# Adjacency block sums made one node tile at a time, and a range check on reciprocals once per batch

## The chip, the core and the metric

The kernel runs on one core of one Trainium2 chip. The metric is the device time of one execution in microseconds, as the median of several runs. A core has five engines with instruction queues of their own: TensorE (PE in the profile; PEld is its loading of weights), VectorE (DVE), ScalarE (ACT), GpSimd (POOL) and SyncE (SP), which issues nearly all DMA transfers here. Each works through its queue in order and waits on semaphores for the others.

## What is computed

Sixteen batches of 1024 nodes with 256 channels go through an attention layer whose queries come from a weighted adjacency, and then through two graph convolutions. Cut to what matters:

```
c    = mean of x over channels
A    = |abs(sigmoid(c_j - c_i) - 0.5) - 0.5| * 2          # likeness of nodes
q    = relu((x^T @ (adj * A_sym)) * para)                  # queries
k, v = x @ kv_w
x1   = layernorm(x + softmax(q k^T * scale) v)             # 4 heads of 64
h    = relu(x1 w1_loop + adj (x1 w1_neigh) + b1)
h    = relu(h w2_loop + adj (h w2_neigh) + b2)
out  = layernorm(x1 + (x1 + h) / 2)
```

All is float32. The adjacency, 1024 x 1024, is the same for all batches.

## The kernel before

**Tiles.** A node tile is 128 nodes; there are eight. Most work tiles are "rows" of 128 partitions x 1024 floats, from a pool of 25 with a tag of their own (`row_tile`). The transposed adjacency is kept as four blocks of 512 x 512. Blocks (0,0), (1,0) and (1,1) stay on chip in `half_adj`, four node tiles of 512 columns each (index k, 0 to 3). Block (0,1) starts out in two row tiles (`rows01`), two node tiles in each, and is stored to memory in batch 1.

**Stages of a batch.** The attention of a batch has four units (two pairs of heads x two halves of the query nodes). A unit computes scores (TensorE, line 596), exponentials (ScalarE, line 599), the running sum of the eight exponential tiles (VectorE, lines 603 and 605), transposes and reduces that sum to `den_part` (lines 607 and 609), and multiplies with the values (TensorE, line 616). `add(u)` then folds the denominators with a small product into PSUM (`den_ps`, line 628, on TensorE), takes reciprocals (line 632), updates a running minimum and maximum of all denominators (lines 633 and 634), scales the output and adds it to x (lines 636 to 639). The minimum and maximum are tested at the very end of the kernel: only if a denominator has left a safe range are all batches redone in a slower, guarded way.

Between the units of batch b stands other work in an order that is written out by hand: after unit 0 the inner product of the convolution of batch b-1 (`gap0`: `c1.inner`, t_ps, line 714), then `att.add(0)`, so `den_ps` follows t_ps on TensorE; after unit 1 the convolutions themselves (`gap1`); after unit 2 the convolution's end (`gap2`). After unit 3 come the queries, keys and values of batch b+1 (`q.step`, line 549; `kv.run`, lines 399 to 434), then the normalization of batch b (`norm.scale`, `norm.spread`), then the next batch's unit 0.

**Block sums.** From batch 2 on, two convolutions of neighbouring batches are done together as one blocked matrix product with seven products instead of eight (`Joined`). Its adjacency operands include four sums of blocks (1, 3, 2, 4, in order of making), which do not change and are made once. `adj_sums(rows01, h)`, lines 196 to 208, makes them for two node tiles at a time: four subtractions of 128 x 1024 on VectorE, each with a store of 512 KB to the memory blocks `far_adj`. It is called twice, both times in batch 1: with h = 0 in the convolution, as a function called after the first four products (line 1020), and with h = 1 behind the next batch's keys and values and ahead of `norm.scale` (line 1109). From batch 2 on the sums are fetched back in every batch.

**Getting the blocks.** The adjacency's node tiles are loaded in blocked form by `adj_blocked` (line 210) and transposed by `turn_adj` (line 951) on VectorE, two transpositions of 512 columns for each tile: tiles 0, 1 and 2 in the opening, while TensorE computes the first queries, and 3 to 7 at the end of batch 0. Tiles k and 4 + k are both needed before the sums for index k can be made. In the opening GpSimd also scales five weight tiles (lines 150 and 152).

**Queues.** Every engine follows the order of the program. SyncE issues a DMA only when its data is ready and its buffer free, and what is behind it waits. The last queries' step of a batch (`q.step(3)`) needs the weighings and sums of `q.pair(3)`, which VectorE makes after `att.add(3)`.

Of the kernel before, what the change touches and what calls it, by code (L numbers as in the profile page):

```python
# [18 lines left out]
def kernel(  # L19
# [31 lines left out]
    nc = tc.nc  # L51

    B, N, C = x.shape
# [10 lines left out]
    EPS2 = EPS / 2.25  # L64
    QSCALE = (1.0 + 1e-06) / (math.sqrt(HD) + 1e-06)

    DEN_MIN = 1e-25
    DEN_MAX = 1e28
    ROWS = 25
    S = 32  # L70
    NB = N // S
# [27 lines left out]
    def row_tile(name):  # L99
        return work.tile([P, N], F32, tag="row", name=name, bufs=ROWS)  # L100
# [62 lines left out]
    for a in range(1, Q):  # L163
        nc.vector.tensor_copy(fold[:, a, :], fold[:, 0, :])

    den_min = const.tile([P, N // S], F32, name="den_min")
    nc.gpsimd.memset(den_min, 1.0)
    den_max = const.tile([P, N // S], F32, name="den_max")
    nc.gpsimd.memset(den_max, 1.0)

# [19 lines left out]
    def of_rows(rows, k):  # L190
        return rows[k // 2][:, ts(k % 2, FB)]
# [1 line left out]
    def adj_block(i, j, k, rows01):  # L193
        return of_rows(rows01, k) if (i, j) == (0, 1) else half_adj[i, j][:, k, :]

    def adj_sums(rows01, h):

        names = (1, 3, 2, 4)
        w11, w21, w22 = (half_adj[ij][:, 2 * h:2 * h + 2, :] for ij in ((0, 0), (1, 0), (1, 1)))
        w12 = rows01[h].rearrange("p (k n) -> p k n", k=2)  # L200
        t = {n: row_tile(f"adjT_{n}_{h}") for n in names}
        v = {n: t[n].rearrange("p (k n) -> p k n", k=2) for n in names}
        nc.vector.tensor_sub(v[1], w12, w11)
        nc.vector.tensor_sub(v[3], w22, w12)
        nc.vector.tensor_sub(v[2], w22, v[1])
        nc.vector.tensor_sub(v[4], w21, v[2])
        for n in names:
            nc.sync.dma_start(out=far_adj[n][h], in_=t[n])

    def adj_blocked(mt):  # L210
        t = row_tile(f"adjB_{mt}")
        for a in range(Q):
            nc.sync.dma_start(
                out=t[a * S:(a + 1) * S, :].rearrange("k (bn r) -> k bn r", r=S),
                in_=adj[:, mt * P + a * S:mt * P + (a + 1) * S].rearrange("(bn k) r -> k bn r", k=S))
        return t
# [39 lines left out]
    def join(part):  # L256
        nc.vector.tensor_add(part[:, 0, :], part[:, 0, :], part[:, 1, :])
# [317 lines left out]
    class Attention:  # L575
# [6 lines left out]
        def __init__(self, b, xB, qT, kT, v):  # L582
            self.b, self.xB, self.qT, self.kT, self.v = b, xB, qT, kT, v
            self.part, self.o = {}, {}

            self.sums = small.tile([P, NC, NB], F32, tag="sums", name=f"sums_{b}", bufs=2)

        def scores(self, u):
# [33 lines left out]
        def add(self, u):  # L622

            b, (pair, j) = self.b, UNITS[u]
            half = FB // S
            pd = bank_psum(f"den_ps_{b}_{u}")
            den = pd[:, 0:2 * half]
            nc.tensor.matmul(den, fold.rearrange("p a k -> p (a k)"), self.part.pop(u), start=True, stop=True)  # L628
            rden = small.tile([P, half], F32, tag="rden", name=f"rden_{b}_{u}", bufs=2)
            for s in range(2):  # L630
                rows = slice(s * HD, (s + 1) * HD)
                nc.vector.reciprocal(rden[rows, :], den[rows, ts(s, half)])
            nc.vector.tensor_tensor(den_min, den_min, den, ALU.min)
            nc.vector.tensor_tensor(den_max, den_max, den, ALU.max)
            o = by_node(self.o.pop(u))
            nc.vector.tensor_mul(o, o, rden.unsqueeze(2).to_broadcast([P, half, S]))
            dst = by_node(self.xB[pair][:, ts(j, FB)])
            nc.vector.tensor_add(dst, dst, o)
            nc.vector.tensor_reduce(self.sums[:, pair, ts(j, half)], dst, AX.X, ALU.add)
            if u == len(UNITS) - 1:  # L640
                join(self.sums)

    def safe_attention(b, xb, qT, kT, v):

# [271 lines left out]
    def run():  # L916
# [14 lines left out]
        sum_key_weights()  # L931
        q.load_para()
        blocked = load_blocked(1, "1")
        tiles = {mt: adj_blocked(mt) for mt in range(3)}
        load_weights()

        def first_weights():
# [22 lines left out]
        for t in range(NT):  # L960
            if t + 3 < NT:
                q.weigh(t + 3)
            q.step(t)
            if t == 4:
                xB = load_blocked(0, "a0")
                ready = {}
                ready["xT"] = channel_major(blocked, "xT_1")
                turn_adj(range(3))
        qT = q.end()
        convs = {}  # L970
        coming = None
        for b in range(B):
# [25 lines left out]
            def weigh_first():  # L998
                q.times_adj(0)
                q.times_adj(TJ)  # L1000
                q.right(0)

            def gap1():
                for t in (0, TJ):
                    q.load(t)
                if both:
                    both.fetch(1, 4)
                    both.run({1: (lambda: q.left(nc.gpsimd),),
                              2: (lambda: att.add(1),),
                              6: (lambda: q.likeness(0), lambda: c3 and c3.moments()),  # L1010
                              7: (lambda: q.likeness(TJ),),
                              5: (weigh_first,),
                              4: (lambda: c3 and c3.finish(out[b - 3]),),
                              3: (c1.turn_blocks,)})
                else:
                    q.left(nc.gpsimd)
                    for t in (0, TJ):
                        q.likeness(t)
                    store("01", rows01)
                    c1.first(rows01, lambda: (att.add(1), adj_sums(rows01, 0), weigh_first()))  # L1020
                    c1.turn_blocks()

            def gap2():
# [36 lines left out]
            if more and not c1:  # L1060
                xT = ready["xT"]
                for t in range(3, NT):
                    q.load(t)
                for t in range(3, NT):
                    q.likeness(t)
                tiles[3] = adj_blocked(3)
                q.times_adj(3)
                q.step(0)
                q.times_adj(4)
                q.step(1)  # L1070
                att.add(3)
                for mt in range(4, NT):
                    tiles[mt] = adj_blocked(mt)
                q.load_para()
                q.times_adj(5)
                q.step(2)
                q.step(3)
                norm.mean()
                q.times_adj(6)
                q.times_adj(7)  # L1080
                q.step(4)
                norm.squares()
                norm.sum_squares()
                q.step(5)
                q.step(6)
                norm.variance()
                xB = load_blocked(b + 1, f"a{b + 1}")
                q.step(7)
                qT = q.end()
                load_next()  # L1090
                norm.scale()
                norm.spread()
                turn_adj(range(3, NT))
                kT, v = keys(b + 1, xT), values(b + 1, xT)
            elif more:
# [12 lines left out]
                if not c2:  # L1108
                    adj_sums(rows01, 1)
                norm.scale()  # L1110
                norm.spread()
            else:
                c2.load_h1()
                c2.load_x()
                both.fetch(2, 3)
                c1.inner()
                both.left(nc.gpsimd)
                both.fetch(1, 4)
                both.run({1: (lambda: att.add(3),), 2: (norm.mean, norm.squares, norm.sum_squares), 7: (norm.variance,),
                          5: (norm.scale, norm.spread)})  # L1120
                c1.turn(0)
                c2.last()
                c1.turn(1)
# [20 lines left out]

    good = small.tile([P, 2], F32, tag="good", name="good", bufs=1)
    ext = small.tile([P, 2], F32, tag="ext", name="ext", bufs=1)
    nc.vector.tensor_reduce(ext[:, 0:1], den_min, AX.X, ALU.min)
    nc.vector.tensor_reduce(ext[:, 1:2], den_max, AX.X, ALU.max)
    nc.vector.tensor_single_scalar(good[:, 0:1], ext[:, 0:1], DEN_MIN, op=ALU.is_ge)
    nc.vector.tensor_single_scalar(good[:, 1:2], ext[:, 1:2], DEN_MAX, op=ALU.is_le)  # L1150
    nc.vector.tensor_mul(good[:, 0:1], good[:, 0:1], good[:, 1:2])
    pn = bank_psum("good_ps")
    nc.tensor.matmul(pn[0:1, 0:1], good[:, 0:1], ones_sb, start=True, stop=True)
# [56 lines left out]
```

## Time and profile before

| what | value |
|---|---|
| median of three runs | 2174.52 us (2174.29 to 2175.86) |
| the profiled execution | 2174.29 us |
| its span, first to last instruction | 2172.4 us |
| busy: TensorE, VectorE, ScalarE, GpSimd | 99%, 87%, 47%, 17% of the span |
| mean granted TensorE clock | 0.998 |
| HBM read and written | 238.16 MB and 46.46 MB, 131 GB/s |
| sum of exponentials (lines 603 and 605) | 571.3 us of VectorE |
| minimum and maximum (lines 633 and 634) | 12.1 and 11.5 us of VectorE, 64 each |
| block sums (lines 203 to 206) | 10.7 us of VectorE, 8 instructions |

The page gives busy time per engine, then the span in 40 slices, DMA queues, the chain of work that ended last, and the costliest groups of instructions. A timeline lists instructions in order of time: start, length, engine, line, operation, output and inputs, shapes, and in brackets how long the engine idled before it and who ended that. Times in a timeline are counted from the start of the span. [...]A list of waits gives the total, the number and the longest. The granted clock is the share of TensorE's full clock that it was given.

### The profile page before, as it was taken

The numbers are of one execution on the slowest core, as the hardware profiler recorded it, in microseconds if no ns is written. First come the engines' busy times: TensorE is split into PE (matmuls) and PEld (weight loads), VectorE is DVE, ScalarE is ACT, GpSimd is POOL, SyncE is SP. The second block draws the span as 40 slices with busy tenths as digits, with TensorE's granted clock in tenths as the row PEclk, the third lists the DMA queues.
The fourth block names the chain that finished last, engine by engine and source line by source line (L and its number), as shares of the span: only waits on it lengthen the run. The fifth ranks groups of instructions, "written<-read, shape, count | busy, mean of one in ns | idle before, by whom it ended". The sixth has DMA issues, their size and how long they took to land.

```text
span 2172.4 us, 23124 instructions
## 1 busy us (share of the span) xinstructions
PE 2155.6 (99%) x8054; PEld 1026.6 (47%) x8054; DVE 1893.7 (87%) x2431; ACT 1027.7 (47%) x1346; POOL 368.2 (17%) x210
## 2 busy tenths in 40 slices
PE   9999999999999999999999999999999999999997
PEld 5344444544444444444444445454454544544354
DVE  4978988898998989989899898999989899898965
ACT  4744545535455453445444454445543445535411
POOL 1011120221303113031120301203022130221021
PEclk9999999999999999999999999999999999999999
DMA  9393563746557374583655626556374653743342
GB/s 230 95 139 116 140 175 89 119 153 122 149 125 144 124 121 155 125 164 102 113 158 130 163 88 114 172 122 155 97 111 166 121 155 113 121 149 82 117 138 96
DMA packets 610619, 286.22 MB, mean 132 GB/s; under 512 B 504640, under 2 KB 569024, under 8 KB 610496
## 3 DMA queue, kind: packets, MB, share of 16 engines
q1 hardware_dynamic: 610224, 284.15, 55.0%
q8 instruction: 65, 1.06, 0.2%
q14 instruction: 58, 0.48, 0.1%
q10 hardware_dynamic: 272, 0.52, 0.1%
HBM read 238.16 MB, written 46.46 MB: 131 GB/s over the span
## 4 chain that ended last, share of the span: by engine, by line
PE 97%; DVE 2%; ACT 0%; DMA 0%; issue 0%; SPq 0%; POOLq 0%; DVEq 0%; POOL 0%
PE s L596 20%; PE av L616 20%; PE hu_ps L875 17%; PE g_ps L549 16%; PE v_ps L363 5%; PE k_ps L408 4%; PE t_ps L714 3%; PE h_ps L782 3%; PE hu_ps L721 2%; PE g_ps L476 2%; PE h_ps L783 2%; DVE acc L605 1%; PE h_ps L736 1%; PE u_ps L765 1%; PE k_ps L353 1%; PE den_ps L628 0%
## 5 line engine op out<-in xcount | busy, mean ns | idle before, releaser
L599 ACT ACTIVATE pr<-s 128x1024 f32<-128x1024 f32 x512 | 476.4, 1054 | 180.0 <-PE s L596 179.9
L605 DVE TENSOR_TENSOR acc<-acc,pr 128x1024 f32<-128x1024 f32 x384 | 494.4, 1288 | 40.7 <-DVE acc L605 0.5
L596 PE MATMUL s<-qT,kT 64*128 64x512 f32 x2048 | 458.8, 598 | 0.7 <-ACT qT L483 0.7
L616 PE MATMUL av<-pr,v 128*64 128x512 f32 x2048 | 453.6, 595 | 0.0
L596 PEld LDWEIGHTS s<-qT,kT 64*128 64x128 f32 x2048 | 191.8, 186 | 237.1 <-ACT pr L599 109.5
L616 PEld LDWEIGHTS av<-pr,v 128*64 128x64 f32 x2048 | 141.4, 137 | 300.0 <-issue 283.9
L329 POOL TENSOR_TENSOR rstd<-rstd,neg_half 128x32 f32<-128x32 f32 x16 | 87.1, 5441 | 1108.6 <-DVE rstd L327 1108.6
L462 ACT ACTIVATE wg<-c_row,c_col 128x1024 f32<-128x1024 f32 x128 | 147.0, 1148 | 73.0 <-DVE accB L607 54.2
L468 DVE SCALAR_TENSOR_TENSOR wg<-wg,adj 128x1024 f32<-128x1024 f32 x128 | 149.9, 1211 | 13.8 <-ACT wg L463 13.8
L875 PE MATMUL hu_ps<-adj,R 128*128 128x512 f32 x360 | 158.3, 596 | 0.0
L463 ACT ACTIVATE wg<-wg 128x1024 f32<-128x1024 f32 x128 | 135.4, 1058 | 4.1
L317 ACT ACTIVATE sq<-xB_a 128x1024 f32<-128x1024 f32 x32 | 33.8, 1057 | 190.0 <-DVE xB_a L312 188.8
L363 PE MATMUL v_ps<-kvw_sb,xT 128*128 128x256 f32 x512 | 120.2, 379 | 0.1
L549 PE MATMUL g_ps<-wg,S 128*128 128x512 f32 x224 | 116.7, 603 | 0.0
L363 PEld LDWEIGHTS v_ps<-kvw_sb,xT 128*128 128x128 f32 x512 | 97.2, 190 | 38.4 <-issue 21.0
L549 PE MATMUL g_ps<-T,S 128*128 128x512 f32 x224 | 114.4, 592 | 0.0
L549 PE MATMUL g_ps<-wg,x 128*128 128x512 f32 x224 | 109.0, 599 | 0.0
L875 PE MATMUL hu_ps<-adjT,t 128*128 128x512 f32 x240 | 105.7, 592 | 0.0
L875 PEld LDWEIGHTS hu_ps<-adj,R 128*128 128x128 f32 x360 | 67.3, 190 | 78.9 <-issue 76.8
L603 DVE TENSOR_TENSOR acc<-pr,pr 128x1024 f32<-128x1024 f32 x64 | 76.9, 1201 | 24.1 <-ACT pr L599 24.1
L607 DVE STREAM_TRANSPOSE accB<-acc 128x1024 f32<-128x1024 f32 x64 | 79.7, 1245 | 3.1
L609 DVE TENSOR_REDUCE den_part<-accB 128x32 f32<-128x1024 f32 x64 | 78.1, 1220 | 2.2
(187 smaller groups left out, 2862.7 us busy)
## 6 DMA issues: line engine op xcount, KB each, us to landing
adj<-in_adj_dram SPq DMA_DIRECT2D x128, 512.0 KB, 4.7
adj<-adjT SPq DMA_DIRECT2D x120, 512.0 KB, 10.2
para<-in_L_gnn_para_dram SPq DMA_DIRECT2D x32, 512.0 KB, 3.5
xB_a<-in_x_dram SPq DMA_DIRECT2D x128, 128.0 KB, 4.2
x1d<-xB_a SPq DMA_DIRECT2D x128, 128.0 KB, 3.4
x<-x1d SPq DMA_DIRECT2D x16, 1024.0 KB, 16.9
xB<-in_x_dram SPq DMA_DIRECT2D x120, 128.0 KB, 4.4
x<-in_x_dram SPq DMA_DIRECT2D x15, 1024.0 KB, 7.3
```

The source lines that it names most:

```text
L329: nc.gpsimd.tensor_tensor(self.rstd, self.rstd, neg_half, ALU.pow)
L363: nc.tensor.matmul(pv[:, ts(i, C)], xT[:, cc, ts(g * per + i, P)], kvw_sb[:, cc, C:2 * C], start=(cc == 0), stop=(cc == NC - 1))
L408: nc.tensor.matmul(dst, self.a[n], self.w[n], start=not again, stop=True, skip_group_check=again)
L462: nc.scalar.activation(wg, self.c_row, AF.Abs, bias=self.c_col[:, t:t + 1], scale=-1.0)
L463: nc.scalar.activation(wg, wg, AF.Tanh, scale=-0.5)
L468: nc.vector.scalar_tensor_tensor(wg, wg, 1.0, self.adj.pop(t), op0=ALU.add, op1=ALU.mult)
L549: nc.tensor.matmul(self.p[n], x_n[:, k, :], w_n, start=(k == 0), stop=(k == TJ - 1))
L596: nc.tensor.matmul(ps[:, ts(s, FB)], self.kT[rows, pair, ts(mt, P)], self.qT[rows, pair, ts(j, FB)], start=True, stop=True)
L599: nc.scalar.activation(pr, ps, AF.Exp)
L605: nc.vector.tensor_add(acc, acc, pr)
L616: nc.tensor.matmul(pav[s * HD:(s + 1) * HD, :], self.v[:, mt, pair * P + s * HD:pair * P + (s + 1) * HD], self.pr[mt][:, ts(s, FB)], start ...
L875: nc.tensor.matmul(dst, self.x[n][:, k, :], half_adj[w][:, k, :] if w else of_rows(rows, k), start=(start and k == 0), stop=(k == TJ - 1), ...
```

## The change

The range check now looks at the reciprocals. Each batch keeps the reciprocals of its four units in one small tile of 128 x 64; when the last unit has been added, right behind `join(self.sums)`, one reduction takes their minimum and one their maximum into a column for that batch. The two updates in every unit go, and so do two memory fills in the opening.

`adj_sums` now takes one node tile (k) at a time: four subtractions of 128 x 512 into the halves of two row tiles, and four stores of 256 KB. It is called for tile 0 in the opening, behind the transpositions; for tiles 1 and 2 in batch 1's convolution; and for tile 3 behind its keys and values. For that the opening loads and transposes tiles 0, 4 and 1 in place of 0, 1 and 2, and batch 0's end transposes 2, 3, 5, 6 and 7. The second row tile of block (0,1) is therefore taken from the pool at the end of batch 0 and not in the opening.

```
-    def adj_sums(rows01, h):
-        names = (1, 3, 2, 4)
-        w11, w21, w22 = (half_adj[ij][:, 2 * h:2 * h + 2, :] for ij in ((0, 0), (1, 0), (1, 1)))
-        w12 = rows01[h].rearrange("p (k n) -> p k n", k=2)
-        t = {n: row_tile(f"adjT_{n}_{h}") for n in names}
...
-        nc.vector.tensor_sub(v[4], w21, v[2])
-        for n in names:
-            nc.sync.dma_start(out=far_adj[n][h], in_=t[n])
+    def adj_sums(rows01, k):
+        w11, w21, w22 = (half_adj[ij][:, k, :] for ij in ((0, 0), (1, 0), (1, 1)))
+        w12 = of_rows(rows01, k)
+        t13, t24 = (row_tile(f"adjT_{n}_{k}") for n in (13, 24))
+        t = {1: t13[:, 0:FB], 3: t13[:, FB:N], 2: t24[:, 0:FB], 4: t24[:, FB:N]}
+        nc.vector.tensor_sub(t[1], w12, w11)
+        nc.vector.tensor_sub(t[3], w22, w12)
+        nc.vector.tensor_sub(t[2], w22, t[1])
+        nc.vector.tensor_sub(t[4], w21, t[2])
+        for n in t:
+            nc.sync.dma_start(out=far_adj[n][k // 2][:, ts(k % 2, FB)], in_=t[n])
...
+            self.rden = small.tile([P, len(UNITS) * FB // S], F32, tag="rden", name=f"rden_{b}", bufs=2)
...
-            rden = small.tile([P, half], F32, tag="rden", name=f"rden_{b}_{u}", bufs=2)
+            rden = self.rden[:, ts(u, half)]
...
-            nc.vector.tensor_tensor(den_min, den_min, den, ALU.min)
-            nc.vector.tensor_tensor(den_max, den_max, den, ALU.max)
...
                 join(self.sums)
+                nc.vector.tensor_reduce(rden_min[:, b:b + 1], self.rden, AX.X, ALU.min)
+                nc.vector.tensor_reduce(rden_max[:, b:b + 1], self.rden, AX.X, ALU.max)
...
-        tiles = {mt: adj_blocked(mt) for mt in range(3)}
+        tiles = {mt: adj_blocked(mt) for mt in (0, TJ, 1)}
...
-                turn_adj(range(3))
+                turn_adj((0, TJ, 1))
+                adj_sums(rows01, 0)
...
-                    c1.first(rows01, lambda: (att.add(1), adj_sums(rows01, 0), weigh_first()))
+                    c1.first(rows01, lambda: (att.add(1), adj_sums(rows01, 1), adj_sums(rows01, 2), weigh_first()))
...
-                tiles[3] = adj_blocked(3)
+                tiles[2] = adj_blocked(2)
...
-                for mt in range(4, NT):
+                for mt in (3, 5, 6, 7):
...
-                turn_adj(range(3, NT))
+                turn_adj((2, 3, 5, 6, 7))
...
                 if not c2:
-                    adj_sums(rows01, 1)
+                    adj_sums(rows01, 3)
```

At the end of the kernel the test compares the smallest and largest reciprocal with 1e-28 and 1e25, where before it compared the smallest and largest denominator with 1e-25 and 1e28.

More of the change, by code (lines that the diff above doesn't have):

```diff
@@ L65 @@
     QSCALE = (1.0 + 1e-06) / (math.sqrt(HD) + 1e-06)
-    DEN_MIN = 1e-25
-    DEN_MAX = 1e28
+    RDEN_MIN = 1e-28
+    RDEN_MAX = 1e25
     ROWS = 25
@@ L164 @@
         nc.vector.tensor_copy(fold[:, a, :], fold[:, 0, :])
[L166 to L169, printed above, removed]
+    rden_min = const.tile([P, B], F32, name="rden_min")
+    rden_max = const.tile([P, B], F32, name="rden_max")
     half_adj = {(0, 0): const.tile([P, TJ, FB], F32, name="adjT_00"),
@@ L194, in adj_block @@
         return of_rows(rows01, k) if (i, j) == (0, 1) else half_adj[i, j][:, k, :]
-    def adj_sums(rows01, h):
-        names = (1, 3, 2, 4)
-        w11, w21, w22 = (half_adj[ij][:, 2 * h:2 * h + 2, :] for ij in ((0, 0), (1, 0), (1, 1)))
-        w12 = rows01[h].rearrange("p (k n) -> p k n", k=2)
-        t = {n: row_tile(f"adjT_{n}_{h}") for n in names}
[L202 to L206, printed above, removed]
-        for n in names:
-            nc.sync.dma_start(out=far_adj[n][h], in_=t[n])
+    def adj_sums(rows01, k):
[9 more added lines that the diff above has]
+            nc.sync.dma_start(out=far_adj[n][k // 2][:, ts(k % 2, FB)], in_=t[n])
     def adj_blocked(mt):
@@ L1146 @@
     ext = small.tile([P, 2], F32, tag="ext", name="ext", bufs=1)
[L1147 to L1150, printed above, removed]
+    nc.vector.tensor_reduce(ext[:, 0:1], rden_min, AX.X, ALU.min)
+    nc.vector.tensor_reduce(ext[:, 1:2], rden_max, AX.X, ALU.max)
+    nc.vector.tensor_single_scalar(good[:, 0:1], ext[:, 0:1], RDEN_MIN, op=ALU.is_ge)
+    nc.vector.tensor_single_scalar(good[:, 1:2], ext[:, 1:2], RDEN_MAX, op=ALU.is_le)
     nc.vector.tensor_mul(good[:, 0:1], good[:, 0:1], good[:, 1:2])
```

## The prediction

> **What bounds the kernel now.** I read the page's busy shares first, then the list of waits for TensorE alone, then the chain in order of time, then timelines around each place where that chain leaves TensorE, and last the tables of windows for the granted clock. The profiled execution took 2174.29 us (span 2172.4, 1.9 outside it); the median of the runs is 2174.52, 0.23 above, so a gain read from this trace carries over to the median as it stands.
>
> ```profile
> PE 2155.6 (99%) x8054; PEld 1026.6 (47%) x8054; DVE 1893.7 (87%) x2431; ACT 1027.7 (47%) x1346; POOL 368.2 (17%) x210
> ```
>
> ```profile
> PE den_ps L628 <- DVE den_part L609: 3.1, 2, 2.3
> ```
>
> TensorE is full. Taking time off VectorE (87%) buys nothing as such: only TensorE's own waits can be won. All its waits on other engines are the 3.1 us shown, in two pieces, and some 3 us of small ones that the edit does not touch (the warm-up, the first scores, the last uT). From batch 2's convolution on, the chain is TensorE without a gap for thirteen batches of 133.2 us each. So everything is decided at the two waits for a denominator. The larger one opens batch 2; VectorE's timeline there (start, length, what; idle before it and who ended that):
>
> ```profile
> 265.42 0.69 DVE L429 TENSOR_TENSOR kT<-ksnap,k_ps 128x512 f32<-128x512 f32 x1 [1.33 <-PE k_ps L408]
> 266.03 1.22 DVE L203 TENSOR_TENSOR adjT<-adjT,adjT 128x1024 f32<-128x1024 f32 x1
> 267.16 2.29 DVE L204 TENSOR_TENSOR adjT<-adjT,adjT 128x1024 f32<-128x1024 f32 x1
> 269.38 1.21 DVE L205 TENSOR_TENSOR adjT<-adjT,adjT 128x1024 f32<-128x1024 f32 x1
> 270.69 1.23 DVE L206 TENSOR_TENSOR adjT<-adjT,adjT 128x1024 f32<-128x1024 f32 x1
> 271.84 2.35 DVE L334 TENSOR_TENSOR xB_a<-xB_a,rstd 128x1024 f32<-128x1024 f32 x2
> ```
>
> GpSimd's timeline, TensorE's timeline, and the table of windows (after each stretch and its length: busy us and count of PE, PEld, DVE, ACT, POOL, then the granted clock, the DMA share and GB/s):
>
> ```profile
> 266.73 1.64 POOL L430 TENSOR_TENSOR kT<-ksnap 128x512 f32<-128x512 f32 x1
> ```
>
> ```profile
> 281.99 3.84 PE L714 MATMUL t_ps<-w1n_sb,x1T 128*128 128x128 f32 x32
> 288.14 0.41 PE L628 MATMUL den_ps<-den_part,fold 128*128 128x32 f32 x2 [2.32 <-DVE den_part L609]
> 288.48 8.83 PE L596 MATMUL s<-qT,kT 64*128 64x512 f32 x32
> ```
>
> ```profile
> 290.00:291.00 1.00, 1.00 (x6) 0.48 (x4) 0.97 (x2) 0.68 (x1) 1.00 (x1) 0.50 0.94 89
> ```
>
> VectorE waits for TensorE until 265.42 and then works without a pause until the denominators' partial sum ends at 288.09. In between stand the block sums of two node tiles, from 266.03 to 271.84: 5.81 us. TensorE is done with t_ps and waits 2.32 us. Then the scores take 8.83 us where undisturbed ones take 7.14 (at 671.78, and in batch 1 at 216.00): the last row shows a granted clock of 0.50 in one of the three windows so slowed, 290 to 293. The stall thus costs twice.
>
> **The change, part by part.** The order of instructions on TensorE and ScalarE is unchanged; VectorE and SyncE change.
>
> *Batch 1's keys: one node tile instead of two.* Four half-width subtractions take the place of the 5.81 us. The keys' own block sums have the same four-step pattern at that width:
>
> ```profile
> 185.86 0.68 DVE L387 TENSOR_TENSOR K<-xT 128x512 f32<-128x512 f32 x1
> 186.46 0.68 DVE L388 TENSOR_TENSOR K<-xT 128x512 f32<-128x512 f32 x1
> 187.06 0.69 DVE L389 TENSOR_TENSOR K<-xT,K 128x512 f32<-128x512 f32 x1
> 187.78 0.69 DVE L390 TENSOR_TENSOR K<-xT,K 128x512 f32<-128x512 f32 x1
> 188.39 0.71 DVE L620 STREAM_TRANSPOSE o<-av 128x512 f32<-128x512 f32 x1
> ```
>
> From first start to next start 2.53 us. Before, one step was held up: L204 to L205 is 2.22 us against 1.13 for L203 to L204, because GpSimd's addition, which reads SBUF, ran from the end of L203 to 268.37. GpSimd will ask at the same 266.73 (its power ends then), now in the second subtraction, so I charge the same 1.09: 3.62 in all. Gain 5.81 - 3.62 = 2.19 us (3.28 if the two miss each other, 1.1 if GpSimd's read came between twice). A check from a steady batch, where no sums stand there: L429 to the end of both scalings is 4.70 us (669.30 to 674.00); here it would be 0.61 + 3.62 + 2.27 = 6.50, 1.80 more. In that batch the partial sum ended at 687.98 and den_ps started unhindered at 689.54, so slack is 1.5 and some 0.3 us of stall remains. Both sums agree: stall down by 2.19, 0.1 to 0.3 left.
>
> *The clock.* The slow scores cost 8.83 - 7.14 = 1.69 us. [...]The rows show the half clock right behind this stall, and none behind the 0.78 us stall at 215.66 (scores after it: 7.14). I go by the rows: with 0.1 to 0.3 us of stall, the 1.69 goes too. Sum 2.19 + 1.69 = 3.88; if the stall vanished, den_ps starting 3.67 us after t_ps as in the steady batch, it would be (288.48 - 281.99 - 3.91) + 1.69 = 4.27.
>
> *Batch 1's convolution: two node tiles, eight half-width subtractions for four full ones.* 2 x 2.53 = 5.06 against 4.66 us (191.79 to 196.45): +0.40, less 0.20 for the minimum and maximum gone just before. Queued behind: the first weighing, right(0), the h1 transposition, then the sum of exponentials, which starts at 203.87 after VectorE has idled 1.07 us for ScalarE. That idle time hides the 0.20; uncovered it would lengthen the 0.78 us stall one to one. That stall itself stays: from 203.87 it is nine serial steps of VectorE to 215.61, behind ScalarE's first exponentials. On SyncE eight stores of half the size stand for four, ahead of h1's stores, which wait for VectorE until 202.8 anyway.
>
> *The opening: four subtractions and four stores more.* VectorE's last transposition ends at 41.5 and qT waits for TensorE:
>
> ```profile
> 40.19 1.30 DVE L958 STREAM_TRANSPOSE adjT<-adjB 128x512 f32<-128x512 f32 x2 [0.94 <-DMA adjB<-in_adj_dram]
> 48.95 1.23 DVE L482 TENSOR_TENSOR qT<-g_ps,para 128x1024 f32<-128x1024 f32 x1 [7.46 <-PE g_ps L476]
> ```
>
> 2.5 us fit into 7.46. But GpSimd scales five weights there (41.25 to 45.73, 0.85 each). No row shows that kind of GpSimd operation beside such a subtraction[...]. By the row of free time the sums end at 44.0[...]. Either way before 48.95: cost 0[...]. The four stores stand behind x's blocked loads on SyncE (issued until 50.6) and ahead of a row that waits for ScalarE until 64.17; 1 MB then delays nothing that is awaited. The third tile loaded (now node tile 1) has the same size and place as the one before. Batch 0's ten later transpositions stay ten, with 4 us of VectorE idle behind them (154.20).
>
> *The range check.* Gone: 64 minima and 64 maxima, 23.6 us busy but 0.10 us of stream time each (218.94, 219.04, 219.14), so 0.8 us per batch. Added: two reductions of 64 elements per batch behind the join; nearest row is the reduction of 32 at the end, 0.18 us, so 0.1 to 0.3 each. They stand ahead of the last weighings. In a steady batch the product that needs t12's second half starts at 653.40 and that half is written at 652.37: 1.0 us of cover, against +0.4 - 0.2. Cost 0, gain 0, since VectorE gives nothing to a full TensorE. The two memory fills leave GpSimd's first microsecond, ahead of a warm-up of TensorE that ends before x's first tiles land (7.48): 0.
>
> *Buffers.* The rows' ring is shifted by one to four places until batch 2's convolution and then falls back into step. The new owners are freed earlier or some microseconds ahead of need: the exponentials of batch 1's third unit wait for the new stores, landed by about 202 (a store of 512 KB took 3.2 us), needed from 204.
>
> What is late next: after the shift TensorE runs 3.9 us earlier. The fetched third block sums (issued at 289.5 and 295.5, landed by 306.3) were wanted at 316.5, the weighing's adjacency loads (landed 310.1) at 320.2. Both keep some 6 us.
>
> **Rivals.** (1) The clock stays slow for some reason other than the stall: 2174.5 - 2.2 = 2172.3. [...]against it the rows; 0.06. (2) The h1 rows land earlier, since 1 MB less is stored ahead of them, [...]In before it started at 285.50, against that step's end at 285.55. One hold costs 1.09, leaves a 1.4 us stall, whose effect on the clock the trace does not show (between 0.78 and 2.32): 2171.7 or 2173.4. In the steady batches I looked at the landing always fell into the last step, never before it; 0.12. (3) Slower: the reductions on VectorE's path to the last queries' step. A pair that costs over 1.0 + 0.2 = 1.2 us stalls TensorE in every batch; at 0.6 us more than that, 14 times, it takes back 3.9 and another 4.4 us, near 2179. It needs 0.9 us each where the row has 0.18; 0.03. (4) The sums do not leave the path but move to batch 1's third unit: +0.2 there at most, inside the main case. (5) More than counted, through a vanished stall and other small waits: 2169.9; 0.09.
>
> **How the numbers follow.** Main case, 0.70: 2174.52 - 3.88 = 2170.6, from 2170.2 (no stall) to 2171.2. The range 2169.6 to 2172.5 takes in the runs' own spread (1.6 us over three), rival 1 and the cheaper half of rival 2. A run of this kernel tells about 0.2%, 4.35 us, from no change, so "faster" begins at 2170.17: 0.09 from case 5 and about 0.13 of the main case's edge make 0.22. Slower 0.03. The rest, 0.75, is within 0.2%.
>
> **What would show it.** Right: the denominator's wait in batch 2 at 0.1 to 0.4 us, the scores after it at 7.14, no window of half clock there, the 0.78 wait unchanged, a period of 133.2 us. Wrong: a wait of over 1 us there, half clock without a long stall, qT starting after 49 in the opening, or any new wait of TensorE in the steady batches.

## The result, and the profile after

| | before | after |
|---|---|---|
| time, median | 2173.99 us (22 runs, 2172.48 to 2175.86) | 2170.18 us (22 runs, 2169.85 to 2170.54) |
| profiled execution | 2174.29, span 2172.4 | 2170.13, span 2168.3 |
| wait for a denominator, opening of batch 2 | 2.32 | 0.18 |
| scores behind it | 8.83 | 7.14 |

The ratio is 0.9984, with a 95% interval of 0.9979 to 0.999: 3.81 us by the medians, 4.16 between the two profiled executions. Forecast were 3.88 us and 2170.6. One thing was not seen in advance: before's times lie in groups. Of the largest set of its runs taken beside the experiments (73), 30 lie around 2172.63, 40 around 2174.34 and 3 at 2175.5 to 2175.8; after's lie in one group. So the change gained 2.45 against the first group and 4.16 against the second.

The busy shares and TensorE's wait for the denominators, after:

```profile
PE 2153.5 (99%) x8054; PEld 1024.9 (47%) x8054; DVE 1892.3 (87%) x2343; ACT 1027.7 (47%) x1346; POOL 367.2 (17%) x208
```

```profile
PE den_ps L626 <- DVE den_part L607: 1.0, 2, 0.8
```

VectorE has 88 instructions fewer and only 1.4 us less to do, for 4.1 us of span. The wait went from 3.1 to 1.0 us, and its longest piece is now the 0.8 of batch 1. VectorE's timeline at the keys of batch 1 (start, length, what; a subtraction is listed at 0.68 us but the next one starts 0.60 after it, so what several take is counted from first start to next start):

```profile
265.51 0.69 DVE L426 TENSOR_TENSOR kT<-ksnap,k_ps 128x512 f32<-128x512 f32 x1 [1.33 <-PE k_ps L405]
266.11 0.68 DVE L200 TENSOR_TENSOR adjT<-adjT,adjT 128x512 f32<-128x512 f32 x1
266.72 0.68 DVE L201 TENSOR_TENSOR adjT<-adjT,adjT 128x512 f32<-128x512 f32 x1
267.32 1.76 DVE L202 TENSOR_TENSOR adjT<-adjT,adjT 128x512 f32<-128x512 f32 x1
269.11 0.69 DVE L203 TENSOR_TENSOR adjT<-adjT,adjT 128x512 f32<-128x512 f32 x1
269.72 2.35 DVE L331 TENSOR_TENSOR xB_a<-xB_a,rstd 128x1024 f32<-128x1024 f32 x2
```

GpSimd's addition, which held up one of the four, and TensorE's timeline:

```profile
266.82 1.71 POOL L427 TENSOR_TENSOR kT<-ksnap 128x512 f32<-128x512 f32 x1
```

```profile
282.07 3.84 PE L712 MATMUL t_ps<-w1n_sb,x1T 128*128 128x128 f32 x32
286.09 0.41 PE L626 MATMUL den_ps<-den_part,fold 128*128 128x32 f32 x2 [0.18 <-DVE den_part L607]
286.43 7.14 PE L594 MATMUL s<-qT,kT 64*128 64x512 f32 x32
```

The sums take 266.11 to 269.72, 3.61 us. GpSimd's addition began at 266.82, during the second subtraction, and the third was held: 1.76 instead of 0.68. The scores run at full clock, as the table of windows says too (after the stretch: its length, busy us and count of PE, PEld, DVE, ACT, POOL; then the granted clock):

```profile
290.00:291.00 1.00, 1.00 (x8) 0.53 (x6) 0.97 (x2) 1.00 (x2) 0.94 (x1) 1.00 0.34 37
```

Where did the 4.16 us between the two profiled executions come from? I subtracted the start of each of the 8054 matmuls after from that before. Up to batch 2 they stay within 0.1 us of each other. The gain is 2.05 at den_ps (2.14 of wait, less the 0.09 by which this execution came there later) and 3.75 behind the slow scores. Then two small steps follow that no step of the forecast has: 0.24 at the keys' product at 1458 and 0.09 at the last batch's `sum_ps` at 2074 (times of before).

The opening, GpSimd's timeline (the first two of its five scalings) and VectorE's:

```profile
41.35 0.86 POOL L150 TENSOR_SCALAR w2l_sb<-w2l_sb 128x256 f32<-128x256 f32 x1 [34.13 <-DMA w2l_sb<-in_L_gnn_w_loop_dram]
42.18 0.86 POOL L150 TENSOR_SCALAR w2n_sb<-w2n_sb 128x256 f32<-128x256 f32 x1
```

```profile
41.64 0.66 DVE L200 TENSOR_TENSOR adjT<-adjT,adjT 128x512 f32<-128x512 f32 x1
42.22 0.91 DVE L201 TENSOR_TENSOR adjT<-adjT,adjT 128x512 f32<-128x512 f32 x1
43.05 0.68 DVE L202 TENSOR_TENSOR adjT<-adjT,adjT 128x512 f32<-128x512 f32 x1
43.76 0.69 DVE L203 TENSOR_TENSOR adjT<-adjT,adjT 128x512 f32<-128x512 f32 x1
49.03 1.23 DVE L479 TENSOR_TENSOR qT<-g_ps,para 128x1024 f32<-128x1024 f32 x1 [4.58 <-PE g_ps L473]
```

The sums are done at 44.45, and 4.58 us of the free time are left. The first subtraction ran beside the first scaling without being held at all (0.66 us).

### The profile page after: what moved, and what is told of

Read it like the earlier page. It is cut to its first block, busy times and chain, and to the rows that moved or that the text cites. A ratio compares the mean times of both kernels' runs of the same rounds, so it can differ in the third digit from the quotient of the medians.

```text
span 2168.3 us, 23079 instructions
## 1 busy us (share of the span) xinstructions
PE 2153.5 (99%) x8054; PEld 1024.9 (47%) x8054; DVE 1892.3 (87%) x2343; ACT 1027.7 (47%) x1346; POOL 367.2 (17%) x208
## 4 chain that ended last, share of the span: by engine, by line
PE 97%; DVE 2%; ACT 0%; DMA 0%; issue 0%; SPq 0%; POOLq 0%; DVEq 0%; POOL 0%
PE s L594 20%; PE av L614 20%; PE hu_ps L873 17%; PE g_ps L546 16%; PE v_ps L360 5%; PE k_ps L405 4%; PE t_ps L712 3%; PE h_ps L780 3%; PE hu_ps L719 2%; PE g_ps L473 2%; PE h_ps L781 2%; DVE acc L603 1%; PE h_ps L734 1%; PE u_ps L763 1%; PE k_ps L350 1%; PE den_ps L626 0%
## 5 line engine op out<-in xcount | busy, mean ns | idle before, releaser
L889 ACT COPY snap<-hu_ps 128x512 f32<-128x512 f32 x15 | 8.8, 586 | 150.2 <-PE hu_ps L873 150.2
```

## The experiments

My theory: the time is decided by VectorE's work between the last keys and the denominator's partial sum in the opening of batch 2, which goes one to one into TensorE's wait, and by the clock that a long wait halves. Rivals: the half clock has another cause; or part of the gain comes from the opening, from the convolution, or from the range check. "Before" beside the experiments had a median of 2174.1 to 2174.2.

| run | wait in batch 2 | median us (runs) | smallest to largest |
|---|---|---|---|
| before, again | 2.32 | 2174.12 (13) | 2172.55 to 2176.00 |
| range check alone | 2.31 | 2174.18 (13) | 2172.43 to 2175.72 |
| block sums alone | 0.18 | 2170.81 (21) | 2170.51 to 2172.00 |
| two tiles in the keys | 2.64 | 2174.07 (13) | 2173.63 to 2177.00 |
| two subtractions more | 1.44 | 2171.88 (13) | 2171.27 to 2172.64 |
| six subtractions more | 4.35 | 2176.83 (19) | 2175.99 to 2177.86 |
| no sums in the keys | 0 | 2170.48 (21) | 2170.29 to 2170.78 |
| the same, and no wait in batch 1 | 0 | 2170.43 (21) | 2170.19 to 2170.78 |
| block sums alone, 24 fills | 0.18 | 2170.57 (21) | 2170.32 to 2170.97 |
| block sums alone, 48 fills | 0.2 | 2171.91 (21) | 2170.92 to 2175.47 |
| no sums in the keys, 24 fills | 0 | 2170.61 (21) | 2170.21 to 2171.21 |
| no sums in the keys, 48 fills | 0 | 2171.55 (21) | 2170.89 to 2173.43 |

**Before, again** (no edit).

> The kernel before, unchanged, run again. Its 22 times lie in two groups, 11 at 2172.5 to 2172.8 and 11 at 2173.9 to 2175.9, some 1.6 apart, which is close to the 1.69 us that I charged to the half clock. Theory: the 2.32 us wait is there in every execution, but it halves the clock only in about half of them. Then both groups come back, and the profile of a run near 2172.6 shows the wait at 2.3, the scores behind it at 7.14 and no window of half clock; one near 2174.3 shows 8.8 and the half clock. Rival: the length of the wait itself differs between the groups (2.3 against about 0.7), with the scores at 8.8 in both.

Five times came back at 2172.6, five around 2174.3, three at 2175.6 to 2176.0. The profiled execution was one of the first group (2172.62). Its TensorE timeline and table of windows, against the 8.83 us and the 0.50 of the earlier profile:

```profile
288.31 0.41 PE L628 MATMUL den_ps<-den_part,fold 128*128 128x32 f32 x2 [2.32 <-DVE den_part L609]
288.64 7.14 PE L596 MATMUL s<-qT,kT 64*128 64x512 f32 x32
```

```profile
290.00:291.00 1.00, 1.00 (x8) 0.49 (x6) 0.97 (x2) 1.00 (x2) 1.00 (x1) 1.00 0.84 95
```

The wait is the same 2.32 us, and the clock held. So these two groups are the clock: behind the same stall it was 0.50 in the earlier profile and 1.00 in this one; the end of this section sets the two side by side. 2174.34 - 2172.63 = 1.71 us, where 8.83 - 7.14 = 1.69. The rival, a wait of another length, falls. The 22 times of the result lie 10 and 12 in the two groups, not 11 and 11 as the expectation has it. What the few times at 2175.5 to 2176 have more was in no profiled execution of before and stays open; on record is that their mean granted clock is 0.996, each time, where the other two groups have 0.997 to 0.999.

**Block sums alone, range check alone.** The change with its new range check taken out, and before with it put in:

```diff
+            nc.vector.tensor_tensor(den_min, den_min, den, ALU.min)
+            nc.vector.tensor_tensor(den_max, den_max, den, ALU.max)
...
-                nc.vector.tensor_reduce(rden_min[:, b:b + 1], self.rden, AX.X, ALU.min)
-                nc.vector.tensor_reduce(rden_max[:, b:b + 1], self.rden, AX.X, ALU.max)
```

> The changed block sums with the old range check (64 minima and maxima, no reductions). Theory: all of the gain is in the block sums, so 2170.2, the wait of batch 2 at 0.2, one group of times. Rival: part of the gain comes from the 1.6 us per batch that leave VectorE with the range check; then some 2171 to 2172.

> The old block sums with the new range check alone. Theory: nothing on TensorE's path, so the two groups of before again, near 2172.6 and 2174.2, the wait of batch 2 at 2.3 and the 0.8 one unchanged. Rival: a gain of 0.5 us or more by itself, or a loss in every batch (over 2176) if the two reductions reach the last queries' step.

The range check alone leaves the wait at 2.31 and the groups where they were: 4 times of 13 around 2172.5, 7 around 2174.2, 2 above. The block sums alone take the wait to 0.18, with one group of times. So the wait and the clock are the block sums' doing. But 2170.81 is 0.63 above the change, which my theory had not foreseen. TensorE's timeline of this run at the keys of a steady batch, and that of the change:

```profile
1454.13 2.11 PE L407 MATMUL k_ps<-xT,kvw_sb 128*128 128x512 f32 x4
```

```profile
1454.00 1.88 PE L405 MATMUL k_ps<-xT,kvw_sb 128*128 128x512 f32 x4
```

The four matmuls take 0.23 us longer. The third waits for VectorE to have read `g_ps` into `U` (line 560, 558 in the change): its weight load stands behind 0.79 us of idle time that this ends, 0.56 in the change. VectorE is late there. Followed back along its timeline, the lateness begins 30 us earlier, between two steps of the sum of exponentials:

```profile
1420.62 1.22 DVE L602 TENSOR_TENSOR acc<-pr,pr 128x1024 f32<-128x1024 f32 x1
1421.94 1.23 DVE L604 TENSOR_TENSOR acc<-acc,pr 128x1024 f32<-128x1024 f32 x1
1423.62 5.21 DVE L604 TENSOR_TENSOR acc<-acc,pr 128x1024 f32<-128x1024 f32 x4 [0.46 <-DVE acc L604]
```

From the second line to the third are 1.68 us, where such steps follow each other after 1.32 (first line to second). Nothing in the trace holds the late one up. Such a step, 0.34 to 0.37 late, stands at four places of this run's steady batches. Behind three of them (at 521, 1454 and 1854) TensorE waits at the same product, 0.21 to 0.26 us each time; in the change's steady batches one such step was found, and it costs nothing. Before has one that costs, at 1458: this is the 0.24 above. The range check alone moves it: it wins 0.25 at 1458 and loses 0.34 at 1592. Matmul by matmul, this run falls 0.69 us behind the change in those three waits and 0.08 in the last batch, where the old minima and maxima stand ahead of the sums; so the late steps, and not the range check's own cost, make up nearly all of it.

**Two tiles in the keys.**

```diff
-                    c1.first(rows01, lambda: (att.add(1), adj_sums(rows01, 1), adj_sums(rows01, 2), weigh_first()))
+                    c1.first(rows01, lambda: (att.add(1), adj_sums(rows01, 1), weigh_first()))
...
                 if not c2:
+                    adj_sums(rows01, 2)
                     adj_sums(rows01, 3)
```

> The change with node tile 2 put back from batch 1's convolution into its keys (one tile made in the convolution, two in the keys, as half-width subtractions). Theory: the wait of batch 2 is 0.18 + 2.5 = 2.7 us, so 2170.2 + 2.5 = 2172.7 when the clock holds and 2174.4 when it is halved, both groups seen, the halved one in half of the runs or more. The wait of 0.8 in batch 1 stays, although the convolution has 2.5 us less, because ScalarE's first exponentials set it. Rival: the opening and the convolution gave part of the gain; then it stays below 2172.0. Rival for the clock: the half clock of before had another cause, and all runs are at 2172.7.

```profile
288.65 0.41 PE L626 MATMUL den_ps<-den_part,fold 128*128 128x32 f32 x2 [2.64 <-DVE den_part L607]
288.99 7.14 PE L594 MATMUL s<-qT,kT 64*128 64x512 f32 x32
```

TensorE's timeline shows the wait at 2.64, as expected (0.18 + 2.5), and den_ps 2.56 us later than in the change. This one part of the change, undone, brings the wait back, so the opening and the convolution gave nothing of it. Batch 1's wait stays at 0.78 with four subtractions fewer in the convolution. Two groups came: 7 times at 2173.6 to 2174.1, 5 at 2175.3 to 2175.7, and one time of 2177.0. Both lie about 1.0 above what I expected. In the profiled execution 0.26 of this is a wait behind a late step (at 1721), and 0.9 lies behind the last store: from its issue to the end are 5.5 us, against 4.5 in the change and 4.6 in before. VectorE's semaphore instruction at the branch of the range check comes 4.46 us after that store instead of 2.91. It has no work there; why it comes late was not tried.

**Doses of VectorE's time.** Two, then six subtractions whose result goes nowhere, behind the keys' sums:

```diff
                     adj_sums(rows01, 3)
+                    extra = row_tile("extra")[:, 0:FB]
+                    for _ in range(2):
+                        nc.vector.tensor_sub(extra, of_rows(rows01, 3), half_adj[0, 0][:, 3, :])
```

> The change with two more half-width subtractions behind the keys' sums of batch 1 (their result goes nowhere). Theory: VectorE's time there goes one to one into TensorE's wait, 0.18 + 1.2 = 1.4 us, so 2170.2 + 1.2 = 2171.4; and the clock is halved only if the wait covers more than about half of one window of 3.4 us, so here never: one group of times, scores at 7.14. Rival: any wait of over a microsecond can halve the clock; then a second group near 2173.1. Rival for the path: the wait doesn't follow VectorE one to one; then below 2171.0. The end behind the last store may add up to 0.9 either way, as two tiles in the keys showed (5.5 us there, 4.6 elsewhere).

> The change with six more half-width subtractions behind the keys' sums of batch 1. Theory: the wait is 0.18 + 3.6 = 3.8 us and covers more than half of some window wherever the window stands, so the clock is halved in every execution: 2170.2 + 3.6 + 1.7 = 2175.5 and one group, no time near 2173.8. Rival: the half clock comes by chance, in about six of ten runs whatever the length of the wait (in before, 2.3 us, 46 of 75 runs; with 2.6 us, 6 of 13); then both groups, 2173.8 and 2175.5.

The window of 3.4 us is the length of the half clock in the profile of before (289.72 to 293.13). That about half of it decides is an estimate: if the window falls anywhere against the wait, 46 of 75 halved runs at 2.32 us give 1.82 us, 53% of it. The table at the end of this section has what was measured. TensorE's timeline with two and with six:

```profile
288.14 0.41 PE L626 MATMUL den_ps<-den_part,fold 128*128 128x32 f32 x2 [1.44 <-DVE den_part L607]
288.48 7.14 PE L594 MATMUL s<-qT,kT 64*128 64x512 f32 x32
```

```profile
290.23 0.50 PE L626 MATMUL den_ps<-den_part,fold 128*128 128x32 f32 x2 [4.35 <-DVE den_part L607]
290.66 6.54 PE L594 MATMUL s<-qT,kT 64*128 64x512 f32 x22
```

The window behind the longer wait:

```profile
292.00:293.00 1.00, 1.00 (x4) 0.36 (x4) 1.00 (x1) 0.21 (x1) 0.55 (x1) 0.50 0.66 57
```

With two, VectorE takes 1.33 us more and the wait is 1.44, 1.26 more; with six it takes 4.24 us more (0.71 each instead of the 0.6 that I had counted) and the wait is 4.35, 4.17 more. Each time 0.07 is missing: VectorE's time goes into the wait nearly one to one. With two, all 13 times are under 2172.65, so no second group at 2173.1 or above. The median is 0.48 above what I expected; in the profiled execution 0.26 of it is a late step at the same place as with two tiles in the keys, 1721, and 0.18 lies behind the last store. (That execution is the largest of the 13 because its first tiles of x came 0.8 us late.) With six, all 19 times lie above 2175.9; with the clock held, 2170.2 + 4.2 = 2174.4 would have been seen. Their spread, up to 2177.9, goes with a mean granted clock that falls from 0.998 to 0.996, and its cause stays open. So the share of halved executions, told by their times, depends on the length: none of 13 at 1.44, 40 to 43 of 73 at 2.32, 5 to 6 of 13 at 2.64, all 19 at 4.35. The rival, chance whatever the length, falls.

**No sums in the keys, and batch 1's wait taken away.** Can both waits go? Node tile 1 was moved to the end of batch 0, where VectorE idles 3.99 us, and tiles 2 and 3 to batch 1's convolution. In the second kernel, besides, batch 1's denominator of unit 2 is asked for behind the first score tile of unit 3:

```diff
                 turn_adj((2, 3, 5, 6, 7))
+                adj_sums(rows01, 1)
...
-                if not c2:
-                    adj_sums(rows01, 3)
```

```diff
+                if mt == 0 and early:
+                    early()
...
-                att.scores(u)
+                att.scores(u, (lambda: att.add(2)) if u == 3 and between and not both else None)
```

> The change with the keys' sums of batch 1 taken away altogether: node tile 1 is made at the end of batch 0, behind the last transpositions, where VectorE idles 3.99 us; tiles 2 and 3 in batch 1's convolution. Theory: the wait of 0.18 in batch 2 goes and nothing else changes, 2170.2 - 0.2 = 2170.0. Rival: moved so, the four stores behind it hold up loads of batch 1 on SyncE, or the shifted row buffers make a new wait; then over 2170.5.

> As the run before it, and besides batch 1's denominator of unit 2 is asked for behind the first of eight score tiles of unit 3 instead of ahead of it; VectorE's order stays. Theory: the wait of 0.78 is covered by 0.86 us of score matmuls, so another 0.78 less: 2169.2. Rival: VectorE, which that wait kept in step, is late by the same 0.8 at the next place (the sum of exponentials of unit 3, the last weighings) and TensorE waits there instead; then 2170.0.

In the first the wait is gone and den_ps starts 0.22 us earlier than in the change, but late steps of VectorE take 0.36 at 1321 and 0.34 at 1588, and the time is 2170.48. (An expectation below has 0.26 and 0.57 for the two; matmul by matmul they are 0.36 and 0.34.) The second falls to its rival. TensorE's timeline:

```profile
214.93 1.13 PE L594 MATMUL s<-qT,kT 64*128 64x512 f32 x4
215.99 0.41 PE L628 MATMUL den_ps<-den_part,fold 128*128 128x32 f32 x2
216.33 1.56 PE L594 MATMUL s<-qT,kT 64*128 64x512 f32 x6
...
254.41 2.32 PE L405 MATMUL k_ps<-xT,kvw_sb 128*128 128x512 f32 x4
```

The wait is gone and the scores run 0.72 us earlier than in the first kernel; 40 us on, the keys' four matmuls take 2.32 us instead of 1.88, and their last one starts at 256.14, where it starts at 256.04 in the change. VectorE is the bound of this stretch. The 0.78 was only the place where its lateness showed first.

**Are the late steps at fixed places of VectorE's stream?** 24 or 48 tiny fills were put into the opening of two kernels:

```diff
                 adj_sums(rows01, 0)
+                pad = small.tile([P, 2], F32, tag="pad", name="pad", bufs=1)
+                for _ in range(24):
+                    nc.vector.memset(pad, 0.0)
```

> The changed block sums with the old range check, and 24 tiny fills of a spare tile on VectorE in the opening, where it idles 4.6 us. The same without the fills took 2170.81, 0.63 over the change. Its profile shows four places in the steady batches where one step of VectorE begins 0.34 to 0.37 us late with nothing that delays it; three of them end in a TensorE wait of some 0.2 us at the keys' third product. Theory: these late steps belong to fixed places in VectorE's stream of instructions (before shows them at instructions 1174 and 1561 in two executions), so 24 more instructions ahead move them 24 instructions earlier in the work, to places that cost more or less; the time moves by 0.2 to 0.6 either way and all runs move together. The range check itself is worth 0.1 to 0.2 (the last batch's sums are 0.2 later). Rival: the 0.63 is the range check's own cost, and the fills change nothing: 2170.8.

> As the run before it with 48 fills. Theory: the late steps are at the same instruction numbers and so 48 instructions earlier in the work; 2170.2 to 2170.9 by where they fall. Rival: 2170.8 as without fills.

> The change with no block sums in batch 1's keys (tile 1 behind batch 0, tiles 2 and 3 in the convolution), and 24 fills in the opening. Without fills it took 2170.48 though the wait of 0.18 was gone; two late steps of VectorE (instructions 1356 and 1646) cost 0.26 and 0.57 in the steady batches. Theory: the late steps keep their instruction numbers and fall elsewhere; where they fall harmlessly the time is 2170.2 - 0.3 = 2169.8, at worst 2170.6. Rival: the extra 0.3 belongs to the moved sums; then 2170.5 stays.

> As the run before it with 48 fills. Theory: 2169.8 to 2170.6 by where the late steps fall. Rival: 2170.5.

24 fills moved the late steps. With the block sums alone, of three that cost TensorE something one is left (0.26 at 1854), and the time fell from 2170.81 to 2170.57. With no sums in the keys there are three other places, and 2170.61.

Two executions of before show their late steps at the same instructions, and so do the two kernels of the last experiment. I had counted only instructions that do work, and by that count 24 fills moved the places by 101. Counted from 0 with its waits and branches, as they stand in the trace, the places are exact: every late step above is one of VectorE's instructions 63, 191, 319 and so on, 128 apart. In the fourteen profiled executions two steps of the sum of exponentials follow each other 5376 times; all 41 that do so after 1.6 to 1.8 us instead of 1.32 stand on this grid. (The 182 that follow after 2.2 us do not; they all have GpSimd's additions beside them.) So the grid stays, as I had expected, and what is put ahead decides which step of the work meets it. Not each of its places is late. With other kinds of step on the grid there are 44 late ones, and behind each of them the traces have a packet of 8192 bytes on a DMA queue that they list as "instruction", started within 0.6 to 3.9 us; of 171 steps on the grid that could be compared with others of their kind and were not late, 23 have one within 4 us. So much is counted; what makes a step late was not shown.

48 fills were too many, and show something else. They take 6.05 us where 4.58 were free, and the first scores wait. VectorE's timeline with 48 fills and no sums in the keys, and TensorE's timeline of the two kernels (the second is the block sums alone):

```profile
44.80 5.92 DVE L970 MEMSET pad<- 128x2 f32 x47
50.77 1.22 DVE L479 TENSOR_TENSOR qT<-g_ps,para 128x1024 f32<-128x1024 f32 x1
```

```profile
53.13 7.14 PE L594 MATMUL s<-qT,kT 64*128 64x512 f32 x32 [2.38 <-ACT qT L480]
```

```profile
53.00 8.83 PE L595 MATMUL s<-qT,kT 64*128 64x512 f32 x32 [2.23 <-ACT qT L482]
```

With no sums in the keys VectorE reaches qT 1.74 us later than in the change (49.03), and TensorE's wait grows from 0.69 to 2.38 or 2.23. The clock was halved behind the shorter one and not behind the longer, as in batch 2 at another place of the kernel. So both runs of 48 fall outside what was expected of them, and say nothing on late steps. No version here beats the change.

**Which stalls halve the clock.** The traces answer this too: each lists the steps of the granted clock, with start and length. In before it is full from 6.41 us on, half from 289.72 for 3.413 us, full again from 293.13, and half from 2167.05, at the program's end; after, it is full from 5.74 and half from 2162.97. These steps lie 3.413 us apart or a whole number of times that: 289.72 is 83 times 3.4133 us behind 6.41, 2167.05 is 633 times behind it, and after's 2162.97 is 632 times behind 5.74. In each of the four profiled executions with a half clock ahead of the end it lasts 3.413 us; with 48 fills it begins 14 times 3.4133 us after the start-up's first step to full clock, and the step down at the end stands 631 to 633 times that length after the first step in all fourteen. That first step came between 4.99 and 7.38 us. So I laid a grid of 3.413 us from each trace's own first step and cut the stalls by it. Before, and before again, two windows each (length, then busy us of PE first; the granted clock is the third number from the end):

```profile
286.30:289.71 3.41, 1.57 (x8) 0.98 (x10) 3.33 (x8) 0.63 (x2) 3.10 (x4) 1.00 0.93 29
289.72:293.13 3.41, 3.41 (x10) 1.39 (x8) 3.34 (x4) 2.28 (x3) 1.45 (x1) 0.50 0.93 130
```

```profile
286.80:290.21 3.41, 1.91 (x10) 1.16 (x12) 3.33 (x8) 0.63 (x2) 3.06 (x4) 1.00 0.94 54
290.21:293.62 3.41, 3.41 (x18) 1.37 (x16) 3.35 (x3) 3.41 (x5) 1.12 (x1) 1.00 0.72 116
```

TensorE was idle for 3.41 - 1.57 = 1.84 us of one window in the first, and for 1.51 of one and 0.81 of the window ahead in the second. All profiled stalls of over 1 us between the start-up and the last batch's end:

| execution | stall | idle in the fuller window | granted clock in the next |
|---|---|---|---|
| six subtractions more | 4.35 | 3.24 | 0.50 |
| range check alone | 2.31 | 2.31 | 0.50 |
| block sums alone, 48 fills | 2.23 | 2.23 | 0.50 |
| before | 2.32 | 1.84 | 0.50 |
| two tiles in the keys | 2.64 | 1.53 | 1.00 |
| before, again | 2.32 | 1.51 | 1.00 |
| no sums in the keys, 48 fills | 2.38 | 1.44 | 1.00 |
| two subtractions more | 1.44 | 0.87 | 1.00 |

The stall's length does not sort these eight (2.31 with a half clock, 2.64 and 2.38 without), but its largest share in one window does: behind 1.84 us and more the clock was half in the next window, behind 1.53 and less it was not. If the grid falls anywhere, a limit between these two gives as an estimate 60 to 78% of halved executions for 2.32 us, 70 to 88% for 2.64, none for 1.44 and all for 4.35. Seen were 55 to 59%, 38 to 46% (of 13), none and all, which would suit a limit near the upper end.

## Why the prediction was right

1. *Only the two waits of TensorE matter.* Nearly right. Of 4.16 us between the profiled executions, 2.14 are the wait and 1.69 the clock: 3.83, where I had 3.88. The rest, 0.24 and 0.09, are smaller waits for VectorE that my list didn't have; the 0.24 stood inside the batches that I had called free of gaps. It is a late step of before that the edit only happened to move: luck.
2. *Batch 1's keys, 5.81 to 3.62 us.* Measured 3.61, with the hold by GpSimd in the place expected and at the price taken from before (1.08 against 1.09). The 0.18 us of wait left lies in the 0.1 to 0.3 forecast.
3. *The clock.* I went by the rows, and they decided rightly: with the wait at 0.18 us no half clock is seen and the scores take 7.14. What I had passed over is that the half clock lasts one window of 3.413 us, on a grid that stands differently in each execution, so that the same 2.32 us stall was followed by half clock where 1.84 us of it fell into one window and by full clock where it was 1.51. I took the 1.69 as certain because the profile showed it and none of the three first times (2174.29, 2174.52, 2175.86) was of the other group; the step holds for the halved group alone. Against the other the gain is 2.45. That the medians differ by 3.81, so near to 3.88, is partly luck: 12 of before's 22 times lay outside the lower group, and with 10 the median would have been one of that group, 2.5 to 2.7 us above the change. Rival 1 (2172.3, the clock stays) didn't come.
4. *Convolution, hidden.* The eight subtractions took 5.06 us as forecast, and the wait stayed at 0.78. Two tiles in the keys show from the other side that VectorE's time there doesn't set it.
5. *Opening, cost 0.* The sums ended at 44.45, where 44.0 was forecast; what the scalings may have cost is 0.25 us (the second subtraction took 0.91 instead of 0.66), and by the listed times the first ran beside a scaling unhindered, in 0.66. The 48 fills show what uncovered time costs there: nearly its full length (1.74 us late at qT, 1.69 more of wait), and in one of the two runs the clock on top (scores of 8.83).
6. *Range check, gain 0.* Too small by 0.1: in the last batch TensorE waits for VectorE at the sums' product (2070 in the change), and there the minima and maxima stood ahead: 0.08 to 0.09 us. The two reductions take 0.13 us of the stream each. In the steady batches VectorE frees the keys' bank 0.10 us later than in before, 0.16 us ahead of need, so the pair is covered. The rival that ends slower didn't come.
7. *Rival 2, GpSimd's first R sum ahead of the last step of the sum of exponentials.* It came near: the R sum began at 282.51, three microseconds earlier than in before (285.50), but within that last step, which ended at 283.43 and was not lengthened; the R sum took 2.05 us where it took 1.27 in before.

## What to carry to other kernels

Of a nearly full engine (TensorE, 99%) only the waits are worth winning, and a wait is worth its length only if the engine that ends it has slack behind it; the 0.78 us of batch 1 came back 40 us later, where the keys' four matmuls took 2.32 us instead of 1.88, because VectorE was late throughout. A stall of 2 to 3 us was paid with half clock in some executions only, by how much of it fell into one window of 3.413 us (1.84 us with half clock behind it, 1.51 without): look at single times before taking a profile's slow stretch as certain. Differences of a few tenths between two versions can come from where VectorE's late steps fall, and need not come from what the edit does.

## What the runs showed that I had not expected

- In the traces the granted clock changes at whole multiples of 3.413 us from its first step, which came at 4.99 to 7.38 us. A window of that grid with 1.84 us or more of idle TensorE was followed by one at half clock, at a cost of 1.7 us (scores of 8.83 instead of 7.14 in before); one with 1.53 or less was not. Of the profiled stalls of 2.2 to 2.7 us three had a half clock behind them and three had none.
- In the sum of exponentials, the 41 steps of VectorE that begin 0.35 to 0.44 us late with no wait to explain it all stand at every 128th of its instructions (63, 191, 319 and so on), waits and branches counted. Not each of these is late, and only those with an unbroken chain to TensorE behind them cost anything, 0.2 to 0.4 us.
- The end behind the last store took 4.3 to 4.9 us in thirteen profiled executions and 5.5 in one, with the same work.
